# The tail of a graph layer with a mixture of experts: diagonals on TensorE, a bias on GpSimd, and small steps in larger groups

## The chip, the cores and the metric

The kernel runs on one core of one Trainium2 chip. The metric is the device time of one execution in microseconds (us). The engines are TensorE (PE, with its weight loads as PEld), VectorE (DVE), ScalarE (ACT), GpSimd (POOL) and SyncE (SP), which here only issues DMAs.

## The reference

One graph layer over 12500 nodes with 256 features and 212500 edges:

```python
m = segment_sum(h[src], dst) * rsqrt(deg_in)[:, None]      # h = x * rsqrt(deg_out)
x2 = m @ W_gc + b_gc + (x @ W_res + b_res)
vals, idx = top_k(x2 @ Wg + bg, 2)                         # 2 of 64 experts
gates = softmax(vals)                                      # two gates a node
core = sum over the two experts of  gate * (gelu(x2 @ w1[e] + b1[e]) @ w2[e] + b2[e])
y = x2 + core
z = (y - mean(y, axis=0)) * rsqrt(var(y, axis=0) + eps) * gamma + beta   # over the nodes
out = layernorm(x + z)                                     # over the 256 features
```

The change touches only the last three lines and the gated sum before them: from the moment when every expert's rows lie in memory to the output. That part is called the tail here.

## The kernel before, in words

Nodes are cut into 98 tiles of 128 (the last has 84 rows). `LOADS` groups the tiles into 14 units: twelve of eight tiles, then tile 96 and tile 97 alone. Each tile has two halves `h` of 128 features. The big array `acc2` ([128, 2, 98*128], in SBUF) holds x2 at first with the nodes on the partitions, tile by tile; in the tail each 128x128 block is transposed in place, so that the features come to lie on the partitions.

The experts write their rows to the array `z_d` in HBM, the first expert's of each node in the first half of it and the second expert's in the second.

**Stage one** of the tail (lines 1386 to 1419) goes over the units. SP loads both experts' rows of a unit into `zt` (line 1389, two DMAs of 1 MB; the pool has two buffers, so a load waits until the unit two before it is used up). ACT multiplies the second expert's rows by their gate in place (line 1392). DVE adds the first expert's rows times their gate into `acc2`, one instruction a tile (line 1396), and then adds the second expert's scaled rows for the whole unit (line 1401). PE transposes the sums into PSUM tiles `q` of four blocks (line 1412; five PSUM buffers), DVE takes the statistics of each `q` (line 1417) and ACT copies it back to `acc2` (line 1419). Meanwhile SP prefetches the input `x` of the first units into buffers `z` (line 1426; five buffers).

Between the stages DVE combines the statistics (lines 1433, 1434 and on) into `amp` and `base`, one number for each feature: the normalized value is `amp * y + base`.

**Stage two** (lines 1452 and on) goes over the units again. ACT applies `amp` and `base` to a unit's two halves in `acc2` (line 1457), PE transposes the blocks back to nodes on partitions, two tiles in one `q` (line 1465), DVE adds `q` to `x` (line 1469) and takes the statistics of each row (line 1471). Thirteen small DVE steps a unit (lines 1474 to 1482, 1487, and 194 to 199 in the helper `rsqrt`, which also has one small ACT step at line 193) make the mean and the scale of the row normalization. ACT applies them, one instruction a tile (line 1489); SP stores the unit (line 1492) and then fetches the `x` of five units later into the freed buffer.

The program is written in a framework that orders the instructions of each engine itself, by the dependences and a priority, and sets the semaphores. So the order on an engine is not quite that of the source: the trace shows unit 1's gate instructions ahead of unit 0's copies, and prefetches of `x` between loads of `zt`. Within an engine's final order, each instruction waits for the one before it.

Other names: `gate[:, k, t]` is the gate of the node on this partition in tile `t` for expert `k`; `ident` is the 128x128 identity, `ones_f` a 128x128 tile of ones; T, V, S and GP are TensorE, VectorE, ScalarE and GpSimd.

Of the kernel before, what the change touches and what calls it, by code (L numbers as in the profile page):

```python
# [8 lines left out]
F32 = mybir.dt.float32  # L9
# [4 lines left out]
AF = mybir.ActivationFunctionType  # L14
ALU = mybir.AluOpType
# [4 lines left out]
P = 128  # L20
N = 12500
D = 256
# [3 lines left out]
EPS = 1e-5  # L26
M = 212500
NT = (N + P - 1) // P
# [68 lines left out]
LOADS = [(t, 8) for t in range(0, 96, 8)] + [(96, 1), (97, 1)]  # L97
# [4 lines left out]
def gnn_moe_kernel(  # L102
# [17 lines left out]
    nc = tc.nc  # L120
# [11 lines left out]
    def rows(t):  # L132
        return P if t < NT - 1 else RAG
# [13 lines left out]
    ident = const.tile([P, P], F32)  # L147
# [1213 lines left out]
    with ExitStack() as stack:  # L1361
        one = stack.enter_context(tc.tile_pool(name="f_one", bufs=1))
        two = stack.enter_context(tc.tile_pool(name="f_two", bufs=2))
        xq = stack.enter_context(tc.tile_pool(name="f_x", bufs=5))
        zq_stack = stack.enter_context(ExitStack())
        zq = zq_stack.enter_context(tc.tile_pool(name="f_z", bufs=2))
        ps1 = stack.enter_context(tc.tile_pool(name="f_ps1", bufs=1, space=PSUM))
        ps2 = stack.enter_context(tc.tile_pool(name="f_ps2", bufs=5, space=PSUM))

        gam = one.tile([P, 2], F32)  # L1370
        nc.sync.dma_start(gam, gamma.rearrange("(h p) -> p h", p=P))
        bet = one.tile([P, 2], F32)
        nc.sync.dma_start(bet, beta.rearrange("(h p) -> p h", p=P))


        gate = one.tile([P, 2, NT], F32)
        S.activation(gate[:, 1], less, AF.Exp)
        V.tensor_scalar_add(gate[:, 0], gate[:, 1], 1.0)
        V.reciprocal(gate[:, 0], gate[:, 0])
        V.tensor_mul(gate[:, 1], gate[:, 1], gate[:, 0])  # L1380


        stat = one.tile([P, 2, 25, 6], F32)
        z3 = [z_d[k * NP : (k + 1) * NP].rearrange("(t p) d -> p t d", p=P) for k in range(2)]
        for t0, n in LOADS:
            r = rows(t0)
            zt = zq.tile([P, 2, 8, D], F32, name="zt")
            for k in range(2):
                nc.sync.dma_start(zt[:r, k, :n], z3[k][:r, t0 : t0 + n])
            for i in range(n):  # L1390
                t = t0 + i
                S.activation(
                    zt[:r, 1, i], zt[:r, 1, i], AF.Copy, scale=gate[:r, 1, t : t + 1]
                )
                y = acc2[:r, :, t * P : (t + 1) * P]
                V.scalar_tensor_tensor(
                    y, zt[:r, 0, i].rearrange("p (h d) -> p h d", h=2),
                    gate[:r, 0, t : t + 1], y, op0=ALU.mult, op1=ALU.add,
                )
            y = acc2[:r, :, t0 * P : (t0 + n) * P].rearrange("p h (t d) -> p t h d", d=P)  # L1400
            V.tensor_add(y, y, zt[:r, 1, :n].rearrange("p t (h d) -> p t h d", h=2))
            if t0 == 96:
                continue
            for h in range(2):
                for b in range(0, n, 4) if t0 < 96 else [-1]:
                    q = ps2.tile([P, 4, P], F32, name="q")
                    at = 0
                    for i in range(4):
                        t = t0 + b + i
                        if t < NT:  # L1410
                            r = rows(t)
                            T.transpose(
                                q[:, i, :r], acc2[:r, h, t * P : (t + 1) * P], ident[:r, :r]
                            )
                            at += r
                    q = q.rearrange("p a b -> p (a b)")[:, :at]
                    V.bn_stats(stat[:, h, (t0 + b) // 4], q)

                    S.copy(acc2[:, h, (t0 + b) * P : (t0 + b) * P + at], q)
        xt = {}  # L1420

        def fetch(k):
            if k < len(LOADS):
                t0, n = LOADS[k]
                xt[k] = xq.tile([P, 8, D], F32, name="z")
                nc.sync.dma_start(xt[k][: rows(t0), :n], part_of(x, t0, n))

        for k in range(5):
            fetch(k)

        mv = one.tile([P, 2, 2, 2], F32)
        for h in range(2):
            V.bn_aggr(mv[:, h, 0], stat[:, h, :24])
            V.bn_aggr(mv[:, h, 1], stat[:, h, 24])

        full, rest = 24 * 512 / N, (N - 24 * 512) / N
        mean = one.tile([P, 2], F32)
        var = one.tile([P, 2], F32)
        gap = one.tile([P, 2], F32)
        V.tensor_sub(gap, mv[:, :, 1, 0], mv[:, :, 0, 0])  # L1440
        V.scalar_tensor_tensor(mean, gap, rest, mv[:, :, 0, 0], op0=ALU.mult, op1=ALU.add)
        V.tensor_mul(gap, gap, gap)
        V.tensor_scalar(var, mv[:, :, 0, 1], full, EPS, op0=ALU.mult, op1=ALU.add)
        V.scalar_tensor_tensor(var, mv[:, :, 1, 1], rest, var, op0=ALU.mult, op1=ALU.add)
        V.scalar_tensor_tensor(var, gap, full * rest, var, op0=ALU.mult, op1=ALU.add)
        amp = one.tile([P, 2], F32)
        rsqrt(one, amp, var, "_f")
        V.tensor_mul(amp, amp, gam)
        base = one.tile([P, 2], F32)
        V.tensor_mul(base, mean, amp)  # L1450
        V.tensor_sub(base, bet, base)
        for g, (t0, n) in enumerate(LOADS):
            r = rows(t0)
            z = xt[g][:r, :n]
            for h in range(2):
                y = acc2[:, h, t0 * P : (t0 + n - 1) * P + r]
                S.activation(y, y, AF.Identity, bias=base[:, h : h + 1], scale=amp[:, h : h + 1])
            st = two.tile([P, 8, 6], F32, name="st")
            for i in range(0, n, 2):
                k = min(2, n - i)  # L1460
                q = ps2.tile([P, 4, P], F32, name="q")
                for j in range(k):
                    t = t0 + i + j
                    for h in range(2):
                        T.transpose(
                            q[:r, 2 * j + h], acc2[:, h, t * P : t * P + r], ident
                        )
                zi = z[:, i : i + k].rearrange("p t d -> p (t d)")
                V.tensor_add(zi, q[:r, : 2 * k].rearrange("p a b -> p (a b)"), zi)
                for j in range(k):  # L1470
                    V.bn_stats(st[:r, i + j], z[:, i + j])

            m = two.tile([P, 8], F32, name="m")
            V.tensor_add(m[:r, :n], st[:r, :n, 1], st[:r, :n, 4])
            V.tensor_scalar_mul(m[:r, :n], m[:r, :n], -0.5)
            gap = two.tile([P, 8], F32, name="gap")
            V.tensor_sub(gap[:r, :n], st[:r, :n, 1], st[:r, :n, 4])
            V.tensor_mul(gap[:r, :n], gap[:r, :n], gap[:r, :n])
            ve = two.tile([P, 8], F32, name="ve")
            V.tensor_add(ve[:r, :n], st[:r, :n, 2], st[:r, :n, 5])  # L1480
            V.tensor_scalar(ve[:r, :n], ve[:r, :n], 1.0 / D, EPS, op0=ALU.mult, op1=ALU.add)
            V.scalar_tensor_tensor(
                ve[:r, :n], gap[:r, :n], 0.25, ve[:r, :n], op0=ALU.mult, op1=ALU.add
            )
            rs = two.tile([P, 8], F32, name="rs")
            rsqrt(two, rs[:r, :n], ve[:r, :n], "_t")
            V.tensor_mul(m[:r, :n], m[:r, :n], rs[:r, :n])
            for i in range(n):
                S.activation(  # L1489
                    z[:, i], z[:, i], AF.Identity, bias=m[:r, i : i + 1], scale=rs[:r, i : i + 1]  # L1490
                )
            nc.sync.dma_start(part_of(out, t0, n), z)
            fetch(g + 5)


# [39 lines left out]
```

## Time and profile before

| | |
|---|---|
| median of 3 runs | 3423.75 us (3421.28 to 3424.61) |
| profiled execution, its own time | 3423.65 us |
| span of the profile, first to last instruction | 3421.9 us |
| mean granted TensorE clock over the span | 0.849 |
| busy share of the span | PE 78%, DVE 48%, ACT 21%, POOL 60% |
| tail (first `zt` load to the end) | 3213.1 to 3421.9 us of the span |
| before the tail | edge sums up to about 2200, tables and sorting, experts from about 2340 to 3210 |

How to read the profile's lines. In the stage tables each stretch has its limits in us from the start of the span, its length, then for PE, PEld, DVE, ACT and POOL the busy time with the number of instructions, then the granted clock of TensorE (1.00 is full), the mean busy share of the 16 DMA engines, and GB/s. In the groups a line has the source line, the engine and the operation, output<-inputs by the program's names, the shapes, the number of instructions, then the busy time in us, the mean duration of one in ns, and the idle time before them with what ended it. In the waits a line has who waited for whom, the total in us, how often, and the longest. In the timeline a line has start and length in us and the number of merged instructions; DVE's and ACT's records overlap a little, so what one instruction costs in a row of equal ones is the distance of the starts.

### The profile page before, as it was taken

What the parts mean: (1) busy time and instruction counts of PE and PEld (TensorE: products, weight loads), DVE (VectorE), ACT (ScalarE), POOL (GpSimd) and SP (SyncE); (2) the same over time, 40 slices, a digit from 0 to 9 for tenths busy, and PEclk for the clock granted to TensorE, in tenths of its full rate; (3) what the DMA queues carried; (4) which work ended last, traced back from release to release, by engine and by line L of the source; (5) the groups of instructions that cost most, each with busy time, mean ns of one, the idle gap of its engine ahead of it and who ended that gap; (6) DMA issues with size and microseconds to landing.
All of it is one profiled execution on the core that took longest, in us unless ns stands there. A gap on an engine that the chain in (4) does not pass through costs nothing. (4 is left out here: it accounts for less than half of the span.)

```text
span 3421.9 us, 36966 instructions
## 1 busy us (share of the span) xinstructions
PE 2685.0 (78%) x11059; PEld 1778.3 (52%) x11121; DVE 1641.3 (48%) x6013; ACT 707.9 (21%) x1994; POOL 2051.2 (60%) x2092
## 2 busy tenths in 40 slices
PE   6826777777787777777777778876999999999644
PEld 5612344444454544444444445554778766778533
DVE  9975534455445445545454455664222212222498
ACT  8930010000010000000000000111222211222368
POOL 0038877777777777777777777754555555554100
PEclk8755578888888888888888988888999999999865
DMA  9462244444444444444444444433344444566677
GB/s 356 158 200 77 85 156 123 125 126 127 128 126 126 127 124 126 128 129 126 122 129 126 126 127 130 131 97 119 111 131 126 133 153 154 178 183 203 214 221 238
DMA packets 257102, 498.19 MB, mean 146 GB/s; under 512 B 44567, under 2 KB 169109, under 8 KB 248578
## 3 DMA queue, kind: packets, MB, share of 16 engines
q0 software_dynamic: 98800, 264.95, 26.8%
q1 hardware_dynamic: 144800, 218.02, 19.5%
q10 hardware_dynamic: 13298, 12.80, 1.2%
q8 instruction: 91, 1.49, 0.2%
q14 instruction: 113, 0.93, 0.1%
HBM read 402.59 MB, written 96.44 MB: 146 GB/s over the span
## 5 line engine op out<-in xcount | busy, mean ns | idle before, releaser
L702 POOL DMA_INDIRECT ring<-h_d,src_col x1584 | 1553.8, 981 | 483.3 <-issue 424.6
L716 PE MATMUL p<-ring,o 128*128 128x258 f32 x3168 | 1207.3, 492 | 473.2 <-DMA ring<-h_d,src_col 436.8
L716 PEld LDWEIGHTS p<-ring,o 128*128 128x128 f32 x3168 | 619.0, 227 | 976.8 <-DMA ring<-h_d,src_col 666.0
L694 DVE TENSOR_SCALAR o<-lane,rel 128x128 f32<-128x128 f32 x1584 | 380.8, 303 | 617.4 <-PE p L716 617.3
L1275 PE MATMUL yp<-w,h 128*128 128x256 f32 (+3 forms) x1928 | 432.9, 380 | 0.0
L1231 POOL DMA_INDIRECT xg<-x_d,tables x241 | 233.0, 967 | 333.1 <-PE xtp L1246 219.4
L1259 PE MATMUL hp<-xT,w 128*128 128x384 f32 (+11 forms) x1328 | 399.4, 454 | 1.4 <-DVE xT L1250 1.4
L1275 PEld LDWEIGHTS yp<-w,h 128*128 128x128 f32 (+3 forms) x1928 | 341.3, 181 | 65.0 <-issue 7.3
L751 ACT COPY s<-p 128x258 f32<-128x258 f32 x132 | 49.4, 374 | 1325.1 <-PE p L716 1325.1
L1263 ACT ACTIVATE h<-hp,w 128x384 f32<-128x384 f32 (+11 forms) x332 | 181.2, 546 | 669.6 <-PE hp L1259 668.8
L1259 PEld LDWEIGHTS hp<-xT,w 128*128 128x128 f32 x1328 | 248.0, 191 | 131.6 <-issue 57.0
L1281 POOL DMA_INDIRECT z_d<-yo,tables x241 | 238.1, 988 | 121.9 <-DVE yo L1280 66.1
L1250 DVE COPY xT<-xtp 128x768 f32<-128x768 f32 (+2 forms) x83 | 77.4, 932 | 405.2 <-PE xtp L1246 405.2
L1280 DVE TENSOR_TENSOR yo<-yp,bb 128x256 f32<-128x256 f32 (+3 forms) x241 | 102.0, 423 | 276.3 <-PE yp L1275 268.5
L421 ACT ACTIVATE s_lo<-lane_b,nb 128x128 bf16<-128x128 bf16 x581 | 171.1, 389 | 4.4 <-DVE lo_end L412 1.8
L1016 PE MATMUL tab<-at,vals 128*128 128x512 bf16 x330 | 130.2, 471 | 18.2 <-DVE vals L1009 7.7
L815 DVE TENSOR_TENSOR acc<-q,acc 128x256 f32 x132 | 55.8, 423 | 165.5 <-PE q L792 122.0
L902 PE MATMUL bank<-wcat,acc 128*128 128x320 f32 x392 | 132.6, 464 | 0.0
L907 PE MATMUL bank<-wcat,xT 128*128 128x320 f32 x392 | 124.4, 440 | 0.0
L477 POOL MEMSET room<- 128x1620 int32 x2 | 2.8, 1447 | 192.7 <-DVE r_out L199 192.7
L711 ACT CAST ring<-mark 128x4 f32<-128x4 bf16 x354 | 57.8, 197 | 260.1 <-issue 260.0
L423 PE MATMUL deg<-o_hi,o_lo 128*128 128x98 bf16 x1079 | 79.9, 237 | 24.6 <-DVE o_lo L204 22.1
(280 smaller groups left out, 2583.8 us busy)
## 6 DMA issues: line engine op xcount, KB each, us to landing
w<-in_wpack SPq DMA_DIRECT2D x64, 1026.0 KB
ring<-h_d,src_col POOLq DMA_INDIRECT x1584, 2.8
z_d<-tables SPq DMA_DIRECT2D x98, 256.0 KB
zt<-z_d SPq DMA_DIRECT2D x24, 1024.0 KB
tables<-h_d SPq DMA_DIRECT2D x118, 128.0 KB
xt<-in_x ACTq DMA_DIRECT2D x48, 256.0 KB
x_d<-y SPq DMA_DIRECT2D x48, 256.0 KB
z<-in_x SPq DMA_DIRECT2D x12, 1024.0 KB
```

The lines of the kernel that those rows point to most:

```text
L421: S.activation(s_lo[:, i], lane_b, AF.Sign, bias=nb[:, k, i : i + 1])
L694: o_last[u] = V.tensor_scalar(o_of[u][:, j], lane, rel[:, c : c + 1], None, op0=ALU.is_equal)
L702: i = GP.indirect_dma_start(out=r[:, k, :D], out_offset=None, in_=h_d, in_offset=bass.IndirectOffsetOnAxis(ap=src_col[:, c : c + 1], axis=0),)
L716: i = T.matmul(p_of[g], o_of[v][:, n], r[:, k], start=j == 0, stop=j == GR - 1)
L902: T.matmul(gps[i][:r], acc2[:, k, a : a + r], wcat[:, k], start=k == 0, stop=False,)
L907: T.matmul(gps[i][:r], v["xT"][:, i, k, :r], wcat[:, 2 + k], start=False, stop=k == 1,)
L1016: T.matmul(tab, vals[:r, m], at[:r], start=t0 + i + k + m == 0, stop=t0 + i == NT - 1 and k + m == 2,)
L1231: GP.indirect_dma_start(out=g, out_offset=None, in_=x2_d, in_offset=bass.IndirectOffsetOnAxis(ap=at[:, 0, k : k + 1], axis=0),)
L1259: T.matmul(hp[:, :m], w1[:, c, j * P : (j + 1) * P], xT[:, c, :m], start=c == 0, stop=c == 1,)
L1263: S.activation(h1[:, j, :m], hp[:, :m], AF.Gelu, bias=w[:, 2 * H + 4 * D + j : 2 * H + 4 * D + j + 1],)
L1275: T.matmul(yp[:r], h1[:, j, k * P : k * P + r], w2[:, j], start=j == 0, stop=j == 3,)
L1281: st = GP.indirect_dma_start(out=z_d, out_offset=bass.IndirectOffsetOnAxis(ap=at[:r, 1, k : k + 1], axis=0), in_=yo[:r], in_offset=None, b ...
```

## The change

In stage one the second expert's rows are no longer scaled by ACT and added by DVE. ACT writes the gates of a tile on the diagonal of a 128x128 tile `dg` instead, and PE adds the rows' transposed block times that diagonal into the PSUM tile that holds the transposed block of `acc2`. In stage two ACT no longer applies `amp` and `base`: PE multiplies by a diagonal of `amp` where it transposed before; `base` is added in five of eight sets by GpSimd, to `x` before it is used, and in sets 0, 3 and 6 by another PE matmul with a diagonal of `base`. The units are taken in another order (the first, then the two single tiles, then the rest) and in sets of up to 16 tiles, and the small steps are done once a set. `x` has six buffers instead of five, and the last unit is stored in two halves.

```diff
-        xq = stack.enter_context(tc.tile_pool(name="f_x", bufs=5))
+        xq = stack.enter_context(tc.tile_pool(name="f_x", bufs=6))
...
             for i in range(n):
                 t = t0 + i
-                S.activation(
-                    zt[:r, 1, i], zt[:r, 1, i], AF.Copy, scale=gate[:r, 1, t : t + 1]
-                )
                 y = acc2[:r, :, t * P : (t + 1) * P]
                 V.scalar_tensor_tensor(
                     y, zt[:r, 0, i].rearrange("p (h d) -> p h d", h=2),
                     gate[:r, 0, t : t + 1], y, op0=ALU.mult, op1=ALU.add,
                 )
-            y = acc2[:r, :, t0 * P : (t0 + n) * P].rearrange("p h (t d) -> p t h d", d=P)
-            V.tensor_add(y, y, zt[:r, 1, :n].rearrange("p t (h d) -> p t h d", h=2))
...
+            for b in range(0, n, 4):
+                m = min(4, n - b)
+                dg = two.tile([P, 4, P], F32, name="dg")
+                for i in range(m):
+                    t = t0 + b + i
+                    S.activation(
+                        dg[:r, i, :r], ident[:r, :r], AF.Copy, scale=gate[:r, 1, t : t + 1]
+                    )
+                for h in range(2):
...
+                        T.matmul(
+                            to, acc2[:r, h, t * P : (t + 1) * P], ident[:r, :r],
+                            start=True, stop=False, is_transpose=True,
+                        )
+                        T.matmul(
+                            to, zt[:r, 1, b + i, h * P : (h + 1) * P], dg[:r, i, :r],
+                            start=False, stop=True,
+                        )
...
+        order = LOADS[:1] + LOADS[12:] + LOADS[1:12]
+        sets = [[0], [1, 2], [3, 4], [5, 6], [7, 8], [9, 10], [11, 12], [13]]
...
-            for h in range(2):
-                y = acc2[:, h, t0 * P : (t0 + n - 1) * P + r]
-                S.activation(y, y, AF.Identity, bias=base[:, h : h + 1], scale=amp[:, h : h + 1])
...
+        for h in range(2):
+            V.tensor_scalar_mul(d_amp[:, h], ident, amp[:, h : h + 1])
+            V.tensor_scalar_mul(d_base[:, h], ident, base[:, h : h + 1])
+        base_p = ps2.tile([P, 4, P], F32, name="q")
+        for h in range(2):
+            T.matmul(base_p[:, h], ones_f, d_base[:, h], start=True, stop=True)
+        base_b = one.tile([P, D], F32)
+        S.copy(base_b, base_p[:, :2].rearrange("p a b -> p (a b)"))
+        def with_base(g):
+            if g % 3 and g < len(sets):
+                for u in sets[g]:
+                    t0, n = order[u]
+                    z = xt[u][: rows(t0), :n]
+                    GP.tensor_tensor(
+                        z, z, base_b[: rows(t0), None, :].to_broadcast([rows(t0), n, D]),
+                        op=ALU.add,
+                    )
+        with_base(1)
+        for g, units in enumerate(sets):
+            with_base(g + 2)
+            st = two.tile([P, 16, 6], F32, name="st")
...
+                            T.matmul(
+                                q[:r, 2 * j + h], acc2[:, h, t * P : t * P + r], d_amp[:, h],
+                                start=True, stop=g % 3 != 0,
+                            )
+                            if g % 3 == 0:
+                                T.matmul(
+                                    q[:r, 2 * j + h], ones_f[:, :r], d_base[:, h],
+                                    start=False, stop=True,
+                                )
...
+                    if i == n - 1 or u == 13 and i == 3:
+                        b = 4 if u == 13 and i == n - 1 else 0
+                        nc.sync.dma_start(part_of(out, t0 + b, i + 1 - b), z[:, b : i + 1])
+                fetch(u + 6)
```

The small steps themselves (13 on DVE, one on ACT) are the same instructions, on up to 16 columns where they had up to eight.

More of the change, by code (lines that the diff above doesn't have):

```diff
@@ L1383, in gnn_moe_kernel @@
         stat = one.tile([P, 2, 25, 6], F32)
+        qs = {}
         z3 = [z_d[k * NP : (k + 1) * NP].rearrange("(t p) d -> p t d", p=P) for k in range(2)]
@@ L1399, in gnn_moe_kernel @@
                 )
-            y = acc2[:r, :, t0 * P : (t0 + n) * P].rearrange("p h (t d) -> p t h d", d=P)
-            V.tensor_add(y, y, zt[:r, 1, :n].rearrange("p t (h d) -> p t h d", h=2))
-            if t0 == 96:
-                continue
-            for h in range(2):
[L1405 to L1408, printed above, removed]
-                        t = t0 + b + i
[L1410 to L1415, printed above, removed]
+            for b in range(0, n, 4):
[7 more added lines that the diff above has]
+                for h in range(2):
+                    if t0 != 97:
+                        q = ps2.tile([P, 4, P], F32, name="q")
+                        qs[h] = q
+                    k = t0 % 2 if t0 > 95 else 0
+                    q = qs[h]
+                    for i in range(m):
+                        t = t0 + b + i
+                        to = q[:, i + k, :r]
+                        T.matmul(
[6 more added lines that the diff above has]
+                        )
+                    if t0 == 96:
+                        continue
+                    at = (m + k - 1) * P + r
@@ L1416, in gnn_moe_kernel @@
                     q = q.rearrange("p a b -> p (a b)")[:, :at]
                     V.bn_stats(stat[:, h, (t0 + b) // 4], q)
-                    S.copy(acc2[:, h, (t0 + b) * P : (t0 + b) * P + at], q)
+                    t = t0 + b - k
+                    S.copy(acc2[:, h, t * P : t * P + at], q)
+        order = LOADS[:1] + LOADS[12:] + LOADS[1:12]
+        sets = [[0], [1, 2], [3, 4], [5, 6], [7, 8], [9, 10], [11, 12], [13]]
         xt = {}
         def fetch(k):
-            if k < len(LOADS):
-                t0, n = LOADS[k]
+            if k < len(order):
+                t0, n = order[k]
@@ L1425, in fetch @@
                 xt[k] = xq.tile([P, 8, D], F32, name="z")
                 nc.sync.dma_start(xt[k][: rows(t0), :n], part_of(x, t0, n))
-        for k in range(5):
+        for k in range(6):
             fetch(k)
@@ L1451, in gnn_moe_kernel @@
         V.tensor_sub(base, bet, base)
[L1452 to L1455, printed above, removed]
-                y = acc2[:, h, t0 * P : (t0 + n - 1) * P + r]
[L1457 to L1481, printed above, removed]
@@ new lines, in gnn_moe_kernel @@
+        d_amp = one.tile([P, 2, P], F32)
+        d_base = one.tile([P, 2, P], F32)
+        for h in range(2):
[6 more added lines that the diff above has]
+        S.copy(base_b, base_p[:, :2].rearrange("p a b -> p (a b)"))
@@ new lines, in with_base @@
+        def with_base(g):
[11 more added lines that the diff above has]
+            st = two.tile([P, 16, 6], F32, name="st")
+            if g == 1:
+                V.memset(st, 0.0)
+            at, all_n = 0, 0
+            for u in units:
+                t0, n = order[u]
+                r = rows(t0)
+                z = xt[u][:r, :n]
+                for i in range(0, n, 2):
+                    k = min(2, n - i)
+                    q = ps2.tile([P, 4, P], F32, name="q")
+                    for j in range(k):
+                        t = t0 + i + j
+                        for h in range(2):
+                            T.matmul(
[7 more added lines that the diff above has]
+                                )
+                    zi = z[:, i : i + k].rearrange("p t d -> p (t d)")
+                    V.tensor_add(zi, q[:r, : 2 * k].rearrange("p a b -> p (a b)"), zi)
+                    for j in range(k):
+                        V.bn_stats(st[:r, at + i + j], z[:, i + j])
+                at += n
+            n, r = at, P
+            m = two.tile([P, 16], F32, name="m")
+            V.tensor_add(m[:, :n], st[:, :n, 1], st[:, :n, 4])
+            V.tensor_scalar_mul(m[:, :n], m[:, :n], -0.5)
+            gap = two.tile([P, 16], F32, name="gap")
+            V.tensor_sub(gap[:, :n], st[:, :n, 1], st[:, :n, 4])
+            V.tensor_mul(gap[:, :n], gap[:, :n], gap[:, :n])
+            ve = two.tile([P, 16], F32, name="ve")
+            V.tensor_add(ve[:, :n], st[:, :n, 2], st[:, :n, 5])
+            V.tensor_scalar(ve[:, :n], ve[:, :n], 1.0 / D, EPS, op0=ALU.mult, op1=ALU.add)
@@ L1482, in gnn_moe_kernel @@
             V.scalar_tensor_tensor(
-                ve[:r, :n], gap[:r, :n], 0.25, ve[:r, :n], op0=ALU.mult, op1=ALU.add
+                ve[:, :n], gap[:, :n], 0.25, ve[:, :n], op0=ALU.mult, op1=ALU.add
             )
[L1485 to L1491, printed above, removed]
@@ L1492, in gnn_moe_kernel @@
-            nc.sync.dma_start(part_of(out, t0, n), z)
-            fetch(g + 5)
+            rs = two.tile([P, 16], F32, name="rs")
+            rsqrt(two, rs[:, :n], ve[:, :n], "_t")
+            V.tensor_mul(m[:, :n], m[:, :n], rs[:, :n])
+            at = 0
+            for u in units:
+                t0, n = order[u]
+                r = rows(t0)
+                z = xt[u][:r, :n]
+                for i in range(n):
+                    S.activation(
+                        z[:, i], z[:, i], AF.Identity,
+                        bias=m[:r, at : at + 1], scale=rs[:r, at : at + 1],
+                    )
+                    at += 1
+                    if i == n - 1 or u == 13 and i == 3:
+                        b = 4 if u == 13 and i == n - 1 else 0
+                        nc.sync.dma_start(part_of(out, t0 + b, i + 1 - b), z[:, b : i + 1])
+                fetch(u + 6)
```

## The prediction

> **What bounds the kernel now.** I read the stage table first: the tail in three stretches (columns: length, then busy time and instructions of PE, weight loads, DVE, ACT, POOL, then clock, DMA share, GB/s), with one stretch of the edge stage (1400:1800) beside it.
>
> ```profile
> 3213.00:3327.00 114.00, 41.91 (x196) 37.83 (x196) 100.94 (x180) 67.78 (x151) 0.00 (x0) 0.62 0.86 271
> 3327.00:3408.00 81.00, 45.34 (x196) 34.82 (x196) 75.62 (x305) 70.93 (x124) 0.00 (x0) 0.56 0.69 223
> 1400.00:1800.00 400.00, 309.62 (x1039) 185.10 (x1051) 201.57 (x983) 37.05 (x157) 303.17 (x318) 0.86 0.44 126
> ```
>
> DVE is busy 101 of 114 us in the first stretch (gated sum and column statistics, "stage one") and 76 of 81 in the second (normalization, "stage two"). ACT comes close in stage two, PE is below 60%, POOL does nothing. The groups say what DVE does:
>
> ```profile
> L1396 DVE SCALAR_TENSOR_TENSOR acc<-zt,gate,acc 128x256 f32<-128x256 f32 x98 | 41.4, 479 | 10.1 <-DMA zt<-z_d 9.9
> L1469 DVE TENSOR_TENSOR z<-q,z 128x512 f32<-128x512 f32 (+2 forms) x50 | 32.5, 671 | 5.4 <-PE q L1465 3.4 <-DMA z<-in_x 1.9
> L1417 DVE BATCH_NORM_STATS2 stat<-q 128x6 f32<-128x512 f32 (+1 forms) x50 | 32.1, 678 | 1.1 <-PE q L1412 1.1
> L1457 ACT ACTIVATE acc<-acc,base,amp 128x1024 f32<-128x1024 f32 (+2 forms) x28 | 29.5, 1120 | 1.6 <-DVE base L1451 1.6
> L1401 DVE TENSOR_TENSOR acc<-acc,zt 128x2048 f32<-128x2048 f32 (+2 forms) x14 | 28.2, 2016 | 0.8 <-ACT zt L1392 0.5
> L1474 DVE TENSOR_TENSOR m<-st 128x8 f32<-128x8 f32 (+2 forms) x14 | 2.3, 165 | 6.1 <-ACT z L1489 6.1
> ```
>
> The change deletes L1401 and L1457 and thins out the steps like L1474. But the loads of stage one depend on L1401. SP's waits and the timeline of one load buffer:
>
> ```profile
> SPq L1389 <- DVE acc L1401: 65.8, 11, 7.6
> ```
> ```profile
> 3277.82 5.97 SPq L1389 DMA_DIRECT2D zt<-z_d  x4
> 3277.85 3.68 PE L1412 MATMUL q<-ident,acc 128*128 128x128 f32 x16 [6.11 <-DVE acc L1401]
> ...
> 3282.83 1.97 PE L1412 MATMUL q<-ident,acc 128*128 128x128 f32 x16 [1.31 <-DVE acc L1401]
> ...
> 3286.26 0.51 ACT L1392 ACTIVATE zt<-zt,gate 128x256 f32<-128x256 f32 x1 [0.47 <-DMA zt<-z_d]
> ...
> 3290.55 2.29 DVE L1401 TENSOR_TENSOR acc<-acc,zt 128x2048 f32<-128x2048 f32 x1
> ```
>
> A buffer's load is issued at 3277.82, lands at 3286.26 (8.4 us), and the buffer comes free at 3292.8 (6.6 us later). With two buffers a unit of eight tiles costs half of load plus use. Over the trace L1401 ends at 3235.35 for unit 1 and at 3315.90 for unit 11: 8.05 us a unit. The same lines price PE: 16 records take 3.68 us at half clock, (3.68-0.4)/15 = 0.218 us each, and 1.97 at full, 0.108 each. A real f32 matmul is two records (L1275 has 8 for four matmuls), each of 0.22 us for 256 columns at full clock, so a 128-column one also costs 0.11.
>
> **Stage one.** Removed: 98 ACT scalings (0.41 apart) and 14 L1401. Added: 98 ACT diagonals of 128 columns (0.29 each by ACT's 128x128 row, L421: 171.1/581), 196 matmuls or 392 records. ACT goes from 68 to 57 us of over 90 and hides; were it late, PE's matmuls would wait behind its PSUM copies. DVE falls from 101 to 73 us and stops being the bound. The buffer is now released by PE's last record: 48 records a unit instead of 16 that came after the release. What a record costs is the open number, 0.108 to 0.218; I take the edge stage's clock of 0.86, where PE was busy 77% much as here, so 0.108/0.86 = 0.126. Use is then 48 x 0.126 + 0.4 = 6.4 us, a unit (8.4 + 6.4)/2 = 7.4. Over ten units 10 x (8.05 - 7.4) = 6.5 us less. That meets the DMA limit: 25.7 MB of rows and 4.4 of prefetched x (5.1 before) at 350 GB/s are 86 us, 9 less than the 95 until the last big unit landed (3308). The drain shortens too: before, 3315.9 to 3326.3, when `base` is ready, holds 16 transposes after the release (3.7 us); now only the last statistics remain, 2.6 us, and the same 3.5 us of small steps after them: -4. Stage one: **-10.5**.
>
> Whether PE holds that clock can be read where only transposes run:
>
> ```profile
> 3328.63:3332.04 3.41, 3.39 (x17) 3.31 (x17) 2.37 (x6) 3.41 (x5) 0.00 (x0) 0.50 0.00 0
> 3332.04:3335.45 3.41, 2.38 (x18) 2.14 (x16) 3.41 (x10) 3.41 (x5) 0.00 (x0) 0.89 0.00 0
> 3335.45:3338.87 3.42, 1.39 (x9) 0.92 (x10) 3.42 (x18) 3.42 (x5) 0.00 (x0) 1.00 0.00 0
> ```
>
> A stretch of full PE work lifts the clock to 1.00; it falls again (0.61, then 0.50) after one with 1.39 us of 3.42 busy. The Trainium skill (TensorE: Matmul & The Clock Gate, Part 4: PE-mode transpose) says that transposes do not engage the fast clock; by it a third of stage one's records would not count and the half-clock rival below would hold, near 3440. The row speaks otherwise, so the sum goes by the row.
>
> **Stage two.** Terms, all on DVE's path:
> Start: four diagonals on DVE at 0.24 (L694: 380.8/1584) are 1.0 us; the first PSUM tile needs 16 records at half clock, 3.5 us, plus 0.4. Before, 3.4 us passed from `base` to DVE's first add (3329.7); now 4.9, or 5.8 if `base_p` goes ahead: +2.
> Set 0: its other three tiles of 16 records come 3.5, 1.7 and 1.7 us apart where DVE needs 1.3 (0.64 for the add, 0.33 twice): 2.2 + 0.4 + 0.4 = +3.
> Sets 3 and 6: 2.0 us per PSUM tile at 0.126 against 1.3; five PSUM buffers give PE a lead of some 5 us against an excess of 5.8: +1 each, +2. At half clock it would be +12 each.
> Small steps: 13 per set, 0.078 apart in the timeline, 14 sets to 8: 78 x 0.078 = -6.
> POOL: seven adds of 128x2048. No row shows one. POOL's memset of 1620 columns takes 1.45 us, so one stream of 2048 is 1.8 and three one after the other 5.5; I take two, 3.7. DVE spends 5.9 us on a unit, which covers even the upper end; uncovered, it is 7 x 3.7 = 26.
> POOL against DVE: no row shows both computing. Bounds: 0 and one add per set (8 x 3.7 = 30). I take +2, near 0, by the nearest rows: DVE's add L815 takes 0.423 us where POOL is 76% busy with descriptors, L1280 of the same shape 0.423 where it is 53% busy. The Trainium skill (SBUF — State Buffer, Who interferes with whom) speaks against the change: a DVE instruction with two SBUF inputs and a POOL instruction that reads SBUF exclude each other for a whole instruction. By it each batch of small steps that meets an add would wait for what is left of it: about 8 x 1/3 x 1.85 = 5 us, and the total would be 3 us worse. No run here shows it yet.
> The copy of `base_b` (0.58, ACT) and one memset (0.1) lie beside other work. ACT loses L1457 (29.5) and is no longer beside DVE at the bound; that yields nothing by itself, because DVE was the longer one.
> SP: each `fetch` still queues behind a store; a set of 16 stores later, but six buffers cover that.
> End: DVE's main work ended at 3407.5, the span at 3421.9: 14.4 us. Now 13 dependent small steps (2.5), eight normalizations (3.5), and the last store (4.1, as from 3417.8): 10.1, so -4.
> Stage two: 2 + 3 + 2 - 6 + 2 - 4 = **-1**, rounded terms.
>
> Sum: -10.5 - 1 = -11.5 on the profiled execution's 3423.65 us (span 3421.9 and 1.75 around it; the median of the runs, 3423.75, is the same within 0.1): **3412**.
>
> **Rivals.** *PE at half clock (slower).* At the clock of the old stages, 0.62, a record is 0.174: a unit (8.4 + 8.8)/2 = 8.6, +5.5, less 4 at the drain; stage two's 552 records take 96 us against the 78 that DVE took, +18, +2, -4: about 3441. It decides below a mean clock of about 0.70 (record 0.155), where both stages cancel. For it: 0.62 and 0.56 in the first table. Against: there PE was busy 37 and 56%, now over 80. Chance 0.15.
> *POOL blocks DVE (slower).* One full wait per set, +30 instead of +2: 3440; it decides from 13 us of waiting. Chance 0.11.
> *The loads bound stage one anyway (no change).* If load time rises with the earlier demand, as DMA is at 0.86 already, the 6.5 and part of the drain are lost: 3420. Chance 0.17.
> *All covers hold (much faster).* Record 0.108, unit 7.0, x fetched after the rows, no PE waits: -22 or more, 3400 and below. Chance 0.10.
> The forecast itself, 3404 to 3418, has 0.47.
>
> **How the numbers follow.** About 0.2%, 7 us, is what a measurement here can tell from no change, so the line to faster is 3417. Most of the forecast case and the large gain are faster, 0.55; the rest of it and the no-change case make 0.18; the two slow rivals, with their neighbours, 0.27. The range 3393 to 3440 takes in the slow rivals' nearer half and leaves out about 0.07 below and 0.13 above.
>
> **What would show it.** Stage one's `zt` loads 7.4 us apart, released by PE; granted clock above 0.8; `base` ready near 3316; DVE steps 0.08 apart with no gaps of microseconds beside POOL's adds; 10 us from DVE's last statistics to the end. Wrong if the clock stays near 0.6, or if DVE's small steps stand still while POOL adds.

## The result, and the profile after

The changed kernel takes 3434.57 us (median of 20 runs, 3426.40 to 3439.46); the kernel before took 3423.45 us beside it (20 runs, 3420.32 to 3426.26). The ratio is 1.0031, interval 1.0024 to 1.0038: slower by some 11 us, where 3412 was forecast. The profiled execution took 3429.35 us, 5.7 us more than that of before; it is the third fastest of the 20.

The stage table of the changed kernel, in the columns of the prediction's first view:

```profile
3215.00:3327.00 112.00, 80.57 (x599) 76.34 (x600) 75.61 (x170) 57.42 (x150) 0.59 (x1) 0.85 0.85 269
3327.00:3410.00 83.00, 66.83 (x547) 65.20 (x546) 77.24 (x230) 38.32 (x81) 32.43 (x9) 0.91 0.68 218
3410.00:3428.00 18.00, 0.00 (x0) 0.00 (x0) 6.20 (x25) 12.11 (x25) 0.00 (x0) 0.50 0.52 175
```

PE is busy and its clock is 0.85 and 0.91, so that part came as foreseen, and DVE lost its 25 us of stage one (101 to 76). Yet the stages hardly shrank. With the limits drawn at the first `zt` load, at `base`, at the end of the last row statistics and at the end of the span:

| us | before | after | forecast change | change |
|---|---|---|---|---|
| start of the tail | 3213.1 | 3215.4 | 0 | +2.3 |
| stage one | 113.2 | 108.8 | -10.5 | -4.4 |
| stage two | 81.2 | 90.3 | +3 | +9.1 |
| end | 14.4 | 13.2 | -4 | -1.2 |

The start varies from profile to profile with the stages ahead of the tail, which the change does not touch. Of the rest, stage two is the surprise. DVE's groups of the changed kernel in stage two (3324 to 3415):

```profile
L1519 DVE BATCH_NORM_STATS2 st<-z 128x6 f32<-128x256 f32 x98 | 36.0, 412 | 0.1
L1517 DVE TENSOR_TENSOR z<-q,z 128x512 f32<-128x512 f32 (+2 forms) x50 | 32.4, 668 | 7.3 <-PE q L1512 5.0 <-POOL z L1485 2.3
L1524 DVE TENSOR_TENSOR m<-st 128x16 f32<-128x16 f32 (+2 forms) x8 | 12.1, 1509 | 0.1
```

L1524 is the first small step of a set, the same instruction as L1474 before (165 ns). Here its mean is 1509 ns, 10.8 us too much over eight, and it counts as busy time, not as a wait. The timeline of DVE shows two of them:

```profile
3362.85 0.69 DVE L1517 TENSOR_TENSOR z<-q,z 128x512 f32<-128x512 f32 x1 [2.26 <-POOL z L1485]
3363.46 3.86 DVE L1524 TENSOR_TENSOR m<-st 128x16 f32<-128x16 f32 x1
3367.24 0.17 DVE L1527 TENSOR_TENSOR gap<-st 128x16 f32<-128x16 f32 x1
...
3377.83 2.94 DVE L1524 TENSOR_TENSOR m<-st 128x16 f32<-128x16 f32 x1
3380.68 0.17 DVE L1527 TENSOR_TENSOR gap<-st 128x16 f32<-128x16 f32 x1
```

And the timeline of POOL, with start and length of its adds. Adds that follow each other share a line: two small and two large ones in the first, two large ones in the next two.

```profile
3326.41 10.37 POOL L1485 TENSOR_TENSOR z<-z,base_b 128x256 f32<-128x256 f32 x4 [114.39 <-ACT base_b L1477]
3358.26 9.01 POOL L1485 TENSOR_TENSOR z<-z,base_b 128x2048 f32<-128x2048 f32 x2 [21.48 <-DMA z<-in_x]
3371.59 9.13 POOL L1485 TENSOR_TENSOR z<-z,base_b 128x2048 f32<-128x2048 f32 x2 [4.31 <-DMA z<-in_x]
3402.73 4.51 POOL L1485 TENSOR_TENSOR z<-z,base_b 128x2048 f32<-128x2048 f32 x1 [22.02 <-DMA z<-in_x]
```

POOL's pair of adds ends at 3358.26 + 9.01 = 3367.27, the stretched step at 3363.46 + 3.86 = 3367.32; the next pair ends at 3380.72, the step at 3380.77. The other two of the four long ones, 0.55 us at 3336.26 and 4.05 us at 3403.23, end with POOL's adds in the same way. The long instructions beside the adds, L1519 (412 ns) and L1517 with one operand in PSUM (668 ns), are not stretched. So DVE's small steps with two inputs in SBUF stand still while POOL adds, as the prediction named for the case that it is wrong. One gets through: L1537 starts at 3371.64, 0.06 us after an add, and takes 0.16 us.

### The profile page after: what moved, and what is told of

It is laid out like the page before. It is cut to its first block, busy times and chain, and to the rows that moved or that the text cites. A ratio compares the mean times of both kernels' runs of the same rounds, so it can differ in the third digit from the quotient of the medians.

```text
span 3427.6 us, 38468 instructions
## 1 busy us (share of the span) xinstructions
PE 2761.0 (81%) x11873; PEld 1855.7 (54%) x11873; DVE 1619.8 (47%) x5926; ACT 669.9 (20%) x1961; POOL 2085.5 (61%) x2101
## 5 line engine op out<-in xcount | busy, mean ns | idle before, releaser
L1280 DVE TENSOR_TENSOR yo<-yp,bb 128x256 f32<-128x256 f32 (+3 forms) x241 | 102.0, 423 | 276.5 <-PE yp L1275 267.7
L1016 PE MATMUL tab<-at,vals 128*128 128x512 bf16 x392 | 147.5, 469 | 11.2 <-DVE vals L1005 11.2
L815 DVE TENSOR_TENSOR acc<-q,acc 128x256 f32 x132 | 55.8, 423 | 162.5 <-PE q L792 118.2
L1485 POOL TENSOR_TENSOR z<-z,base_b 128x2048 f32<-128x2048 f32 (+2 forms) x9 | 33.0, 3694 | 162.2 <-ACT base_b L1477 114.4
```

The lines of the kernel that those rows point to most:

```text
L1016: T.matmul(tab, vals[:r, m], at[:r], start=t0 + i + k + m == 0, stop=t0 + i == NT - 1 and k + m == 2,)
```

## The experiments

Theory A: POOL's adds block DVE's small steps, and that makes stage two longer. Its rivals: PE's extra matmuls, or x that lands late. For stage one: the two buffers of eight tiles set the pace, against a DMA that is full, or held up by the x between the rows. The first four kernels ran on a chip where the kernel before takes 3424.0 us, the next four on a second and the last four on a third; on those two the kernel before takes 3727.5 and 3727.0 us. Their tails start some 300 us later, so ratios are compared and stages are taken from the profiles.

### POOL's adds left out

`base` is then missing from `x` in five of eight sets; the rest is the changed kernel.

```diff
-            if g % 3 and g < len(sets):
+            if False:
```

> The changed kernel without POOL's seven large and two small adds: base is left out of x in five of the eight sets, all else as it is. Theory A (the loss is DVE's small steps standing still while a POOL add runs): the first small step, L1524, which took 0.55, 3.86, 2.94 and 4.05 us beside POOL's adds, goes back to 0.17 in all eight sets, about 10.8 us less on DVE's path, 2.3 us less of waiting for x, and about 3 us less at the end, where the last set's steps queue on ACT behind the set before; the time falls by 12 to 20 us from 3434.6, to 3415 to 3422. Theory B (stage two is bound by PE's 552 records or by its clock): nothing on PE is taken away, so the time stays above 3430.

Measured: 3421.78 us, ratio 0.9992 (0.9983 to 1.0001), 13 us below the changed kernel. DVE's groups of this kernel in stage two:

```profile
L1519 DVE BATCH_NORM_STATS2 st<-z 128x6 f32<-128x256 f32 x98 | 36.2, 411 | 0.1
L1517 DVE TENSOR_TENSOR z<-q,z 128x512 f32<-128x512 f32 (+2 forms) x50 | 32.5, 670 | 6.0 <-PE q L1512 4.7 <-DMA z<-in_x 1.3
...
L1524 DVE TENSOR_TENSOR m<-st 128x16 f32<-128x16 f32 (+2 forms) x8 | 1.4, 169 | 0.1
```

L1524 is back at 169 ns. Stage two takes 77.2 us instead of 90.3. Of the 13.1 us between them DVE's busy time makes 11.3 (82.3 to 71.0), nearly all of it the 10.8 us of blocked steps; the rest is idle time, above all that L1517 waited 2.3 us for POOL's `z` and now waits 1.3 us for `x` itself. That is Theory A for stage two, by its cause and by its size; PE's extra matmuls are still there, so they are not the loss. The gain in the span is 9.3 and not 13.1, because stage one took 0.9 us more in this profile and the end grew from 13.2 to 16.2 us, where some 3 us less were expected:

```profile
DVE rsq_r_t L194 <- ACT rsq_r_t L193: 6.1, 1, 6.1
```

In the changed kernel this line has 3.2 us. The last set's square root on ACT stands behind the 16 normalizations of the set before. In the changed kernel DVE came later by what POOL cost it, and ACT's queue was shorter by then.

### Each stage of the change alone

The first kernel is that of before with stage one of the change, and everything behind it as it was:

```diff
-                S.activation(zt[:r, 1, i], zt[:r, 1, i], AF.Copy, scale=gate[:r, 1, t : t + 1])
...
-            V.tensor_add(y, y, zt[:r, 1, :n].rearrange("p t (h d) -> p t h d", h=2))
...
+                    S.activation(dg[:r, i, :r], ident[:r, :r], AF.Copy, scale=gate[:r, 1, t : t + 1])
...
+                        T.matmul(to, zt[:r, 1, b + i, h * P : (h + 1) * P], dg[:r, i, :r],
+                            start=False, stop=True)
```

> Stage one of the changed kernel, stage two of the kernel before (five x buffers, POOL idle). Theory C (stage one is bound by its loads in both kernels, so only the drain after the last load is shorter): 3 to 6 us below the kernel before, 3418 to 3421, with loads of a unit still about 8 us apart. The forecast's step (7.4 us a unit): 10 us below, 3413. If the diagonals on PE cost time by themselves (rival of half clock): above 3424.

Measured: 3421.30 us, 0.9994 (0.9985 to 1.0003); stage one 109.5 us, against 113.2 before. The total cannot be told from no change; in the stage the gain is 3.7 us, a third of the forecast one.

The second is the changed kernel with these lines the other way round, so that stage one is that of before.

> Stage one of the kernel before, stage two of the changed kernel with POOL's adds. Theory A: all of the loss is here, 12 to 18 us above the kernel before, 3436 to 3442, since the small gain of stage one is missing. If instead the loss lies in stage one or in the interplay of the two: within 5 us of the kernel before.

Measured: 3439.99 us, 1.0049 (1.0036 to 1.0063): the new stage two costs 16 us here. In its profile the blocked time is 15.0 us, and it falls on other steps: L1511 (the first small step) 3.87 us, L196 3.36, L199 3.94, and L198 4.44, which has one input in SBUF and a constant. Which step is hit, and how many of them in a set, depends on where POOL's adds happen to lie against DVE's steps.

### base by PE, without POOL

```diff
-            if g % 3 and g < len(sets):
+            if False:
...
+        part64 = one.tile([P, P], BF16); V.memset(part64, 1.0 / 64)
+        mix = one.tile([P, D], BF16)      # base in bf16 on 64 partitions, its remainder on the others
...                                        # (the copies that fill it)
+                            if g > 0:
+                                T.matmul(q[:r, 2 * j + h], part64[:, :r],
+                                    mix[:, h * P : (h + 1) * P], start=False, stop=True)
```

> The changed kernel with base added by PE in all sets, POOL idle: in sets 1 to 7 a one-record bf16 matmul (base split into two bf16 parts, on 64 rows each, against a tile of 1/64) follows each f32 one. Three records per 128 columns instead of two; at 0.11 us each that is 0.66 us a tile beside DVE's 0.65. Theory A: as the run without POOL's adds, plus at most 5 us if PE falls behind, 3415 to 3427. Theory B: PE has more records than in the changed kernel, so the time stays at 3434 or rises.

Measured: 3419.74 us, 0.9991 (0.9982 to 1.0000), end 16.2 us as without POOL. Stage two takes 80.6 us in its profile, 3.4 more than without POOL's adds, but there DVE waits 4.9 us for `x` (1.3 without), 1.6 us while `mix` is made, and only 1.9 us for PE (4.7 without). So `base` can be added by PE for nearly nothing, and the POOL adds were not needed to relieve it.

### POOL's adds in pieces of one tile

```diff
-                    GP.tensor_tensor(
-                        z, z, base_b[: rows(t0), None, :].to_broadcast([rows(t0), n, D]), op=ALU.add)
+                    for i in range(n):
+                        GP.tensor_tensor(z[:, i], z[:, i], base_b[: rows(t0)], op=ALU.add)
```

> The changed kernel with each POOL add cut into adds of one tile (128x256, about 0.6 us instead of 4.5), the same sums. Theory A, with the wait lasting until the running POOL instruction ends: a DVE step waits 0.6 us at most at each meeting; several of the ten steps of a set that use the shared port can meet a new piece, so 1 to 2 us for each of the four sets that meet adds; 3424 to 3429, between the changed kernel (3434.6) and the one without adds (3421.8). If the wait were not for one instruction but for the whole of POOL's queued work, or the adds cost by their volume: unchanged at 3434.

Measured: ratio 1.0012 (1.0003 to 1.0021). That lies in Theory A's range (3424 to 3429 is 1.0002 to 1.0016 of 3423.45). But the changed kernel itself, repeated on the third chip, has the same 1.0012 (below), so no gain by the pieces is shown; on this chip the changed kernel was not run. The timeline of DVE where a set of small steps meets a row of 16 pieces:

```profile
3661.96 0.18 DVE L1524 TENSOR_TENSOR m<-st 128x16 f32<-128x16 f32 x1
3662.06 0.74 DVE L1527 TENSOR_TENSOR gap<-st 128x16 f32<-128x16 f32 x1
3662.72 0.77 DVE L1530 TENSOR_TENSOR ve<-st 128x16 f32<-128x16 f32 x1
3663.40 0.75 DVE L1525 TENSOR_SCALAR m<-m 128x16 f32<-128x16 f32 x1
3664.07 0.77 DVE L1528 TENSOR_TENSOR gap<-gap 128x16 f32<-128x16 f32 x1
```

A step no longer waits 4 us once, but each step waits for one piece: they start 0.68 us apart, about the length of a piece (0.69 apart on POOL), against 0.08 without it. The steps lose 13.3 us in all, between the 10.8 and the 16 us of the two profiles of the changed kernel, and stage two takes 90.7 us.

### Loads of four tiles

The same bytes and the same memory, in four buffers instead of two; the rest is the changed kernel.

```diff
-        zq = zq_stack.enter_context(tc.tile_pool(name="f_z", bufs=2))
+        zq = zq_stack.enter_context(tc.tile_pool(name="f_z", bufs=4))
...
-            zt = zq.tile([P, 2, 8, D], F32, name="zt")        # loads and gated sums of a whole unit
...
             for b in range(0, n, 4):
                 m = min(4, n - b)
+                zt = zq.tile([P, 2, 4, D], F32, name="zt")    # loads and gated sums of four tiles
```

> The changed kernel with stage one's loads in units of four tiles and four buffers (the same memory and bytes). Theory C1 (the pair of buffers sets the pace: load plus use, halved): the queue always holds another load, so stage one goes at the DMA rate, 30 MB at 350 GB/s, 86 us instead of some 95 until the last rows land; 6 to 9 us faster than the changed kernel, 3426 to 3429. Theory C2 (the 16 DMA engines are full already): no change, 3434. POOL's waits are still there and vary by some us.

Measured: ratio 0.9961 (0.9947 to 0.9974), 17 us below before in spite of POOL; stage one takes 86.7 us, 22 less than in the changed kernel, where 6 to 9 were expected. The middle of stage one of the changed kernel, and then of this one:

```profile
3230.00:3300.00 70.00, 55.62 (x439) 53.15 (x438) 51.92 (x109) 41.36 (x111) 0.00 (x0) 0.93 0.98 312
```
```profile
3530.00:3580.00 50.00, 46.58 (x384) 43.47 (x383) 46.09 (x96) 35.64 (x97) 0.00 (x0) 1.00 1.10 348
```

At 48 PE records a unit, the first makes 9.1 units in 70 us, 7.65 us each, and the second 8 units in 50, 6.25 us each. PE and DVE are busy 93 and 92% of the time now, PE at full clock, and DMA moves 348 GB/s (a unit's 2.1 MB take 6.0 us at that). In the changed kernel no engine was above 80%, and of the 312 GB/s that DMA moved some 40 went to x. So the engines waited for each other. The edit moved x as well: SP issues its first x load here only at 3592.50, behind the loads of all rows, so the rows of the last big unit have landed 76 us after the first issue, against 95.5 in the changed kernel. The expected 86 us had the 4.4 MB of x among the rows, which is part of why the gain is larger. Whether x alone had a part in it is tried below.

### Both repairs, and one with small last sets

Loads of four tiles and `base` by PE together, both edits as above.

> base by a bf16 matmul in sets 1 to 7, POOL idle (as e4, 3419.7), with the loads of four tiles and four buffers. C1: 6 to 9 us below e4, 3411 to 3414. C2: 3419 to 3420.

Measured: 3700.40 us against 3727.52, ratio 0.9931 (0.9917 to 0.9944): the fastest version here, faster than before by 27 us. On the 3423.45 us of the first chip that ratio is some 3400, 11 us below C1's range. Its stages are 86.8, 76.8 and 16.2 us.

The same with smaller sets at the end:

```diff
-        sets = [[0], [1, 2], [3, 4], [5, 6], [7, 8], [9, 10], [11, 12], [13]]
+        sets = [[0], [1, 2], [3, 4], [5, 6], [7, 8], [9, 10], [11], [12], [13]]
```

> As e7_both, with the last three units as sets of eight tiles instead of one of sixteen and one of eight. Theory D (the end is long because the last set's square root queues on ACT behind the sixteen normalizations of the set before, 6.1 us in the runs without POOL): half of that is left, 3 to 5 us below e7_both, less 1 us for one more batch of small steps on DVE. If the end is set by the last store instead: as e7_both or 1 us above.

Measured: 0.9933 (0.9920 to 0.9947), no gain. DVE's wait for the square root fell from 6.1 to 3.6 us, as Theory D has it, and the end from 16.2 to 14.7; but stage two rose from 76.8 to 77.8.

### Loads of four tiles in the kernel before

```diff
-            zt = zq.tile([P, 2, 8, D], F32, name="zt")       # with its scalings and its L1401 for eight tiles
+            for b in range(0, n, 4):
+                zt = zq.tile([P, 2, 4, D], F32, name="zt")   # the same for four, four buffers
```

> The kernel before, with its rows loaded in pieces of four tiles into four buffers (same bytes, same memory), everything else as it was. Question: do finer loads alone bring the 17 us that they brought the changed kernel (ratio 0.996), or does the changed arithmetic have to come first? D (DVE is the second bound): before, DVE is busy 101 of stage one's 113 us, so finer loads can take away only its idle rest; stage one 103 to 107 us, 6 to 10 us less, ratio 0.9972 to 0.9985. L (loads alone set stage one in both): stage one near 90, 20 us less, ratio 0.994. N (the idle 12 us are start and drain, not loads): within 2 us of before, ratio 0.9994 to 1.0006. I hold D.

Measured: ratio 1.0013 (1.0004 to 1.0022), slower by 5 us; both D and L are wrong on the size, N is nearest. The middle of stage one, before and with the finer loads:

```profile
3230.00:3300.00 70.00, 28.32 (x134) 25.24 (x132) 68.14 (x112) 45.92 (x103) 0.00 (x0) 0.65 1.04 326
```
```profile
3554.00:3606.00 52.00, 23.07 (x96) 18.52 (x96) 48.68 (x85) 33.80 (x73) 0.00 (x0) 0.56 0.93 304
```

DVE is busy 97% in the first and 94% in the second: with the old arithmetic it has no room, and halving L1401 made it dearer (30.1 us for 26 instead of 28.2 for 14). That is half of the 3.8 us by which stage one grew (117.0 against 113.2). So the change's stage one was needed first, and by itself gave 3 us, within the noise; the finer loads by themselves lose 5; together they give over 20.

### x held back

The changed kernel with its two buffers of eight, but no prefetch of x before unit 9's rows have landed.

```diff
+            if t0 == 72:
+                for k in range(6):
+                    early[k] = xq.tile([P, 8, D], F32, name="z")
+                    V.tensor_copy(early[k][:, 0, :1], zt[:, 0, 0, :1])
...                                                    # fetch() then loads x into these buffers
```

> The changed kernel, with the same two buffers of eight tiles, but the prefetches of x held back until the rows of unit 9 have landed (a one-column copy by DVE into each x buffer orders it; six such copies cost about 0.5 us). Question: why did a unit's period stay at 8.0 us instead of 7.4, and why did smaller loads remove 22 us? X (the x loads that slot in between, about 4 of them of 1 MB at 350 GB/s, 3 us each, stretch the loads that follow): stage one 96 to 101 us against 109, total 6 to 12 us less than the changed kernel of this call, unless stage two then waits for x. B (a unit's buffer is freed all at once and DMA stands idle while both buffers are in use; x only filled the holes): stage one stays at 106 to 110, total within 3 us of the changed kernel of this call or up to 8 us worse, as x now lands later. I hold B at 0.55, since in the changed kernel's record DMA moves only 276 GB/s on the mean in stage one against 350 at its full.

Measured: 3740.58 us, 1.0037 (1.0023 to 1.0051), 9 us above the changed kernel beside it; stage one 111.8 us against 107.3. Both lie 1 to 2 us beyond Theory B's range, and opposite to Theory X. Without any x in the way the issues of units 2 to 9 lie 7.70 us apart (3534.08 to 3587.99), as in the changed kernel there (7.69). The 4.5 us more in stage one stand behind the issue of tile 96's rows: 17.0 us from there to `base`, against 12.5. The rate of DMA in 40 slices of 1.8 us, from 3518 to 3590, where only rows are loaded:

```profile
GB/s 20 282 376 350 348 349 349 256 9 73 350 373 349 347 350 349 145 114 371 370 340 335 355 350 108 1 59 287 369 348 349 348 348 224 99 352 369 336 21 81
```

DMA runs at 350 for two units, then stands still for some 3 us. Both buffers are in use then: units 2 and 3 are issued 5.3 us apart, 4 and 5 are 5.9 apart, 6 and 7 again 5.3, but from 3 to 4 it is 8.7 and from 5 to 6 it is 10.9. The prefetches of x had only filled these holes. Finer loads with x still among the rows were not run.

### Finer loads with the old stage two

The first kernel of "each stage alone" (stage one of the change, the rest as before), with the loads of four tiles as above.

> Stage one of the change with the loads in pieces of four tiles and four buffers, then stage two as before (ACT applies amp and base, eight tiles at a time). Question: once stage one is short, does any of the new stage two pay? Sum of stages from the earlier profiles: 86.8 + 81.7 + 14.5 = 183 us against 208.8 of the kernel before: 24 to 27 us less, and 3 us more than the version with all parts and a bf16 base (27 us less, 0.9931). So ratio 0.9930 to 0.9940 for theory S (stages add up), 0.995 or more for theory X2 (the old stage two, with five x buffers and its x now fetched only at the end of stage one, waits for x).

Measured: 3702.82 us, 0.9936 (0.9923 to 0.9950), as theory S has it: stages add up. It cannot be told from the version with both repairs (0.9931), so of that version's 27 us nearly all come from stage one; what the new stage two adds without POOL is within the intervals (in the profiles the tail is 183.6 us here and 179.8 there).

### The changed kernel again

No edit.

> The changed kernel itself again, beside the others of this call, so that they can be compared on one chip. Theory A (POOL's adds block DVE's small steps, how many depends on where they meet): slower than before by 3 to 16 us, ratio 1.001 to 1.0045, with several us of spread between runs. Theory S (a fixed cost of the change): 1.0031 within 0.0007, as in the first measurement.

Measured: 1.0012 (1.0003 to 1.0021), slower again, by 4 us; the interval lies below the first one (1.0024 to 1.0038), so the cost is not fixed. That fits Theory A, but the chip is another one too, and no run separates the two. Its profiled execution (3737.22 us, the longest of its eleven runs) has 16 us of blocked steps where the first profile has 10.8. Some of DVE's small steps in its timeline:

```profile
3672.39 4.41 DVE L198 TENSOR_SCALAR rsq_q_t<-rsq_q_t 128x16 f32<-128x16 f32 x1
3677.31 3.95 DVE L199 TENSOR_TENSOR rs<-rsq_r_t,rsq_q_t 128x16 f32<-128x16 f32 x1
...
3712.34 4.40 DVE L197 TENSOR_TENSOR rsq_q_t<-rsq_q_t,ve 128x16 f32<-128x16 f32 x1
```

POOL's pair runs here from 3672.26 to 3681.23: one set of steps is blocked by both adds, one after the other. That also fits the spread of the changed kernel's first runs, 13 us against 6 before, though no run shows it for them one by one.

## Why the prediction was wrong, by its own steps

**POOL against DVE, the step that failed.** The sum had +2 us, near the lower bound of 0 to 30. It cost 10.8 us in the first profile, 15.0 with the old stage one and 16 in the repeat; in the first, DVE also waited 2.3 us for POOL's add, which had started late because x came late. The value was taken from rows in which POOL was busy with descriptors (L815, L1280); those say nothing of a POOL instruction that reads and writes SBUF. And in both rows one of DVE's operands comes from PSUM, the form that POOL's adds do not stretch either (L1517). So the nearest rows were not near. The rival "POOL blocks DVE" had the right mechanism; its price, one full add per set, was too high, and its point of decision, 13 us of waiting, was nearly met. The rule of the Trainium skill that the prediction set against itself (SBUF — State Buffer, Who interferes with whom) is borne out: the steps with two SBUF inputs wait until the running add has ended (3.86, 2.94, 4.05 us), the ones with an operand in PSUM do not. The same section says that a `tensor_scalar` can take both ports in its fast modes; the 4.41 us of L198 agree. The estimate made by that rule, 5 us, was still too low: it let a third of the sets meet an add and lose 1.85 us each. In the first profile four of eight sets met one and lost 2.7 us on the mean. An add takes 4.5 us, two stand back to back, and in the repeat a set that had waited for one waited for the next too.

**Stage one: -10.5 forecast, -4.4 measured.** The record of 0.126 us (clock 0.86) was right: the clock is 0.85. The drain was right too: from the issue of tile 96's rows to `base` it takes 12.5 us instead of 16.9, 4.4 less where 4 were forecast. So nearly all of the gain is the drain, and next to nothing came of the 6.5 us for the unit period: up to that issue the tail takes 96.2 us in both kernels, and a unit 8.0 us (ten from 3231.8 to 3311.6) instead of 7.4. SP's timeline around units 6 to 9, and PE's at the same time:

```profile
3263.69 6.31 SPq L1390 DMA_DIRECT2D zt<-z_d  x4
3270.04 2.22 SPq L1441 DMA_DIRECT2D z<-in_x  x1
3277.35 10.23 SPq L1390 DMA_DIRECT2D zt<-z_d  x4
3287.63 1.53 SPq L1441 DMA_DIRECT2D z<-in_x  x1
3294.74 1.13 SPq L1390 DMA_DIRECT2D zt<-z_d  x2
```
```profile
3279.59 0.46 PE L1420 MATMUL q<-dg,zt 128*128 128x128 f32 x2 [2.05 <-DMA zt<-z_d]
...
3287.84 0.41 PE L1416 MATMUL q<-ident,acc 128*128 128x128 f32 x2 [1.27 <-DVE acc L1395]
3289.42 0.41 PE L1416 MATMUL q<-ident,acc 128*128 128x128 f32 x2 [1.17 <-DVE acc L1395]
...
3295.82 0.35 PE L1420 MATMUL q<-dg,zt 128*128 128x128 f32 x1 [0.90 <-DMA zt<-z_d]
```

A line "x4" holds the loads of two units, 6 and 7, then 8 and 9; unit 7's are issued at 3269.01, when unit 6's have not yet landed (3272.13). PE first waits for the rows (2.05 us), works through that unit, waits for DVE's sums of the next (1.27 and 1.17) and then for rows again.

The term that was mis-sized is the load. The sum had 8.4 us for load and 6.4 for use. Measured from a unit's first issue to its last landing, and from there to the next issue into its buffer, units 2 to 9 have 9.65 and 6.24 us on the mean: the use was right, and half of the two is 7.9. The kernel before has 9.15 and 7.12, half of them 8.1: the 8.4 came from one load, unit 8's, and unit 9's, issued while unit 8's was under way, took 10.0. The sum could have shown it: with 8.4 and 6.6 its formula gives 7.5 us for the kernel before, where 8.05 was measured. It set a computed period against a measured one; formula against formula is 0.1 us a unit, 1 us in all.

That half of load plus use sets the pace while two buffers are in use fits these means, and fits the experiments (x held back: no change; four smaller buffers: 6.25). The rival "the loads bound stage one anyway" gives the right size for stage one (3420; stage one alone gave 3421.30) and part of the reason: the load did lengthen, by 0.5 us a unit. But DMA was not full (312 GB/s in the middle of the stage, 348 with the finer loads). That the remedy was as large as 22 us was nobody's theory.

**End: -4 forecast, -1.2 measured, +1.8 without POOL.** The sum took the last set's small steps as if ACT were free. ACT's timeline at the end of the changed kernel shows it:

```profile
3410.10 7.97 ACT L1544 ACTIVATE z<-z,m,rs 128x256 f32<-128x256 f32 x16 [1.92 <-DVE m L1537]
3417.97 0.19 ACT L193 ACTIVATE rsq_r_t<-ve 128x8 f32<-128x8 f32 x1
3419.49 4.04 ACT L1544 ACTIVATE z<-z,m,rs 128x256 f32<-128x256 f32 x8 [1.33 <-issue]
```

Sixteen normalizations of the set before take 7.97 us (0.50 each), and the last set's square root is queued behind them. Larger sets delay what stands behind a set on ACT: a cost that the sum did not have. Eight normalizations are 4.04 us, not 3.5; they are 4.04 us in the kernel before too (from 3405.88).

**What was right.** PE keeps its clock, 0.85 and 0.91, so the half-clock rival is out. From `base` to DVE's first add of stage two it is 4.8 us, forecast 4.9. The small steps are 0.08 us apart when nothing blocks them. Set 0 and sets 3 and 6 were forecast at +5 for PE; DVE's waits for PE's tiles are 5.0 us in all, 4.2 of them the start, so they cost 0.8. Without POOL stage two would have been 4.0 us shorter than before; forecast was +1.

**Size and sign.** The profiled executions differ by 5.7 us: +2.3 start, -4.4, +9.1, -1.2. The forecast had -11.5. Of the 17 us between, stage one accounts for 6, stage two for 6 (POOL 11 worse, PE 5 better), the end for 3 and the start of the tail for 2. The measured medians differ by 11 us, within the range given, on the other side of no change. The 5 us between the profiled execution and the median stand in no profile; the repeat, whose profile is of its longest run, lost more to blocked steps (16 us).

## What to carry to other kernels

Work that is moved to POOL is not free because POOL is idle: while it adds in SBUF, DVE's small two-input steps stop, and cutting the add into pieces only spread the wait over more steps here; add a constant row by PE instead, where PE has room. A bound engine that is relieved shows its gain only if the loads can follow: when no engine is above 80% busy and DMA's rate has holes, more and smaller buffers of the same memory are the next thing to try; where DVE was 97% busy they lost 5 us. Before small steps are gathered into larger sets, look at what queues behind a set on the other engine at the very end.

## What was unexpected of the hardware

An add of 128x2048 in f32 takes POOL 4.5 us, and adds of 128x256 follow each other 0.69 us apart; while it runs, a DVE step of 0.17 us with both inputs in SBUF ends 0.03 to 0.05 us after the add does. A step blocked in this way is booked as busy, so it shows in an instruction's mean (1509 ns against 169) and not in the waits. A `tensor_scalar` with one SBUF input was blocked too (4.41 us); a reciprocal with one (L194, 0.25 us beside an add in two of the profiles), statistics, and adds with an operand in PSUM were not (412 and 668 ns, as without POOL). And with PE at 93% busy the granted clock was 1.00, where at 79% it was 0.93 and at 40% 0.65.
